# A gated graph network: the last step of the last pair by halves of the nodes, 1 - z ahead of tanh, one more turn on TensorE

## The chip, the cores and the metric

The kernel runs on one core of a Trainium2 chip. The metric is device time in microseconds for one execution. The core has TensorE (PE, with its weight loads shown apart as PEld), VectorE (DVE), ScalarE (ACT), GpSimd (POOL), and SyncE (SP), whose queue issues every DMA here. The profile records one execution; its span runs from the first to the last instruction.

## The reference, cut to what matters

x is 32 samples of 512 nodes with 128 features, adj a 512 x 512 matrix shared by all. Everything is in float32.

```python
# layer 0: powers of adj up to 3 (both adjacencies are the same adj)
x = layernorm(x + sum_k (adj^k @ x) @ W_k)
# layer 1: five steps of a gated update
h = x
for _ in range(5):
    m  = adj @ h                       # in_matrix and out_matrix are the same
    u3 = h @ u3_w.T + u3_b
    z  = sigmoid(cat(m, m) @ w3_w.T + w3_b + u3)
    r  = sigmoid(cat(m, m) @ w4_w.T + w4_b + u3)
    hv = tanh(cat(m, m) @ w5_w.T + w5_b + ((r * h) @ u5_w.T + u5_b))
    h  = (1 - z) * h + z * hv
out = layernorm(x + h)                 # x here is the output of layer 0
```

## The kernel before

The 32 samples are worked as 16 pairs (q = 0 to 15, b = 0 and 1 within a pair). A pair goes through layer 0 and then through five steps (s = 0 to 4) with its h kept turned, features on the partitions and 512 nodes along the free dimension, in a tile hT of 128 x 512. In each step PE makes u = u3 h (L978; ACT adds the bias, L983, into a uT buffer), then the product of the pair with adj. That product is one of Strassen's seven-product schemes: sums S of blocks of X on POOL (L501), seven products on PE (L514), each taken out of its bank by ACT (L375) or DVE (L379), into m. Then come the gates of each batch (function gates): m with w4, w3 and w5 on PE (L896), additions on DVE (L901, L908), sigmoids on ACT (L903, L910), rh = r h on DVE (L904), rh with u5 on PE into the bank of w5, tanh on ACT (L917), and h + z (hv - h) on DVE and POOL (L929, L931, L933).

For the next product h is needed with nodes on the partitions (X). Most steps turn it by DMA (function turn): a stream transpose of 32 x 32 blocks on DVE (L350), four puts to DRAM (L342), one fetch (L348). The X that comes so lies in blocks, and ACT (two) and POOL (one) copy parts of it into S (L494). ON_PE says how many of a pair's last steps turn h with four PE transposes (L293) and one ACT copy (L1030) instead: one for pair 14, two for pair 15. Where step 4 itself is such a step (pairs 14 and 15), the last update is "quick": 1 - z is a second sigmoid with scale -1 (L922), (1 - z) h and z hv are products on DVE (L924, L926), and function finish adds h0, (1 - z) h and z hv in one PSUM bank with 48 small matmuls for a pair (24 for a batch, L944, with the identity as one operand), which also turns them. Then norm takes the statistics of each of four node blocks on DVE (L304, L305), the scale on POOL (L308 to L313), applies it on ACT (L321; for the very last batch on DVE, L317, with a shorter POOL part), and one DMA stores the sample (L961; L1045 for the other pairs).

No order is written out by hand. Every operation is handed to a Plan with its engine, an estimated duration, the operations it comes after, the buffer slots it takes and gives back, and a key. Plan.run goes through time with these estimates, and whenever an engine is free, gives it the ready operation with the smallest key, provided that its slots are free; ties go to the one that became ready first. The order in which operations leave this run is each engine's instruction order. A pair's keys are KEYS[q] plus 30 plus LONG (19) per step plus an offset for the kind of work: product 0, u 5, gates 10 to 10.8, turning 15. TT_KEY is the key of a set of sums of adj blocks (TT, L243), made once near the start and used by the four-sample product in layer 0. Slots that matter below: 2 rh buffers, 6 uT buffers, 8 PSUM banks, 14 slots "inside", one of which a pair holds from the start of its five steps to their end.

Of the kernel before, what the change touches and what calls it, by code (L numbers as in the profile page):

```python
# [10 lines left out]
AF = mybir.ActivationFunctionType  # L11
ALU = mybir.AluOpType
# [3 lines left out]
NK = 4  # L16
N = NK * P
H = NK // 2
HN = N // 2
R = 32  # L20
NR = P // R
STEPS = 5
ON_PE = {14: 1, 15: 2}
KEYS = [-2.0, 20.0, 50.0, 76.0, 96.0, 132.0, 162.0, 176.0, 194.0, 222.0, 242.0, 278.0, 304.0, 334.0, 350.0, 366.0]
LONG = 19.0
TT_KEY = 33.0
SQ_KEY = 16.0
KEPT = 3
FIRST = 2
# [97 lines left out]
def gnn_resnorm_kernel(  # L127
# [17 lines left out]
    nc = tc.nc  # L145
    NP = x.shape[0] // 2
# [7 lines left out]
    def tiles(tag, n, shape=(P, N), pool=work):  # L154
# [3 lines left out]
        bank=tiles("bank", 8, pool=psum),  # L158
        d=tiles("d", 6, (NR, R, NR, P), dram),
# [8 lines left out]
        hT=tiles("hT", 8),  # L168
        X=tiles("X", 3),
        uT=tiles("uT", 6),  # L170
        rh=tiles("rh", 2),
        z=tiles("z", 3),
        m=tiles("m", 5),
        S=tiles("S", 2, (P, 7, H, P)),
        v=tiles("v", 5),
        two=[None] * 4,
        inside=[None] * 14,
    )
    plan = Plan(slots)

    def chunk(k):
        return slice(k * P, (k + 1) * P)
# [3 lines left out]
    ident = const.tile([P, P], F32, tag="ident", name="ident")  # L186
# [40 lines left out]
    for i, (a, b) in enumerate(((B12, B11), (B22, T[:, 0]), (B22, B12), (B21, T[:, 1]))):  # L227
        emit = lambda i=i, a=a, b=b: nc.vector.tensor_tensor(T[:, i], a, b, ALU.subtract)
# [4 lines left out]
    for i, n, of in (  # L233
# [6 lines left out]
        t = lambda j, i=i, n=n: TT[:, i : i + n, j, :]  # L240
        own = []
        for j, (a, b) in enumerate(((b12, b11), (b22, t(0)), (b22, b12), (b21, t(1)))):
            emit = lambda d=t(j), a=a, b=b: nc.vector.tensor_tensor(d, a, b, ALU.subtract)  # L243
            after = T_sums + own[:2]
# [21 lines left out]
    ready = []  # L266
# [16 lines left out]
    u3s, u5s = plain(u3, "u3s"), plain(u5, "u5s")  # L283
    b3s, b4s, b5s = plain(b3, "b3s"), plain(b4, "b4s"), plain(b5, "b5s")
    ub3s, ub5s = plain(ub3, "ub3s"), plain(ub5, "ub5s")
    hv_b = const.tile([P, 1], F32, tag="hv_b", name="hv_b")
# [8 lines left out]
    def norm(n, name, src_of, dst_of, after, give, key, by_dve=False):  # L295

        mv = small.tile([P, n, 2], F32, tag="mv", name=f"mv_{name}")
        rstd = small.tile([P, n], F32, tag="rstd", name=f"rstd_{name}")
        shift = small.tile([P, n], F32, tag="shift", name=f"shift_{name}")
        got = []  # L300

        def moments(i):
            st = small.tile([P, 6], F32, tag="st", name=f"st_{name}_{i}")
            nc.vector.bn_stats(st, src_of(i))  # L304
            nc.vector.bn_aggr(mv[:, i, :], st)  # L305

        def power():
            nc.gpsimd.tensor_scalar(rstd, mv[:, :, 1], EPS, None, ALU.add)  # L308
            if not by_dve:
                nc.gpsimd.tensor_scalar(shift, mv[:, :, 0], -1.0, None, ALU.mult)  # L310
            nc.gpsimd.tensor_tensor(rstd, rstd, mhalf[:, :n], ALU.pow)  # L311
            if not by_dve:
                nc.gpsimd.tensor_tensor(shift, shift, rstd, ALU.mult)  # L313

        def apply(i):
            if by_dve:
                nc.vector.tensor_scalar(  # L317
                    dst_of(i), src_of(i), mv[:, i, 0:1], rstd[:, i : i + 1], ALU.subtract, ALU.mult
                )
                return  # L320
            nc.scalar.activation(  # L321
                dst_of(i), src_of(i), AF.Identity, bias=shift[:, i : i + 1], scale=rstd[:, i : i + 1]
            )

        for i in range(n):
            got.append(plan("DVE", 0.48, lambda i=i: moments(i), after=after, key=key))
        p = plan("POOL", 1.2 if by_dve else 1.75, power, after=got, key=key)
        engine, us = ("DVE", 0.35) if by_dve else ("ACT", 0.5)
        over = []
        for i in range(n):  # L330
            ends = give if i == n - 1 else []
            over.append(plan(engine, us, lambda i=i: apply(i), after=[p] + over, give=ends, key=key))
        return over
# [89 lines left out]
    for km in range(NK):  # L423
        emit = lambda km=km: transposes(plan[f"ba{km}"], lambda k: at[:, k, chunk(km)])
        take = [("bank", f"ba{km}")] + ([("h0", f"an{km // H}")] if km % H == 0 else [])
        tr = plan("PE", 0.44, emit, after=at_in, take=take, key=SQ_KEY)
        emit = lambda km=km: nc.scalar.copy(an_of(km)[:, km % H], plan[f"ba{km}"])
# [7 lines left out]
    for i, (a, b, op) in enumerate(  # L435
# [7 lines left out]
        emit = lambda i=i, a=a, b=b, op=op: nc.vector.tensor_tensor(an_sum(i)(), a(), b(), op)  # L443
        take = [("h0", f"anS{i // H}")] if i % H == 0 else []
# [14 lines left out]
    t = lambda i: lambda: T[:, i]  # L459
# [9 lines left out]
    dst = lambda i, j: at2[:, i * H : (i + 1) * H, j * HN : (j + 1) * HN]  # L469
    whole = lambda bank: bank.rearrange("p (k c) -> p k c", k=H)  # L470
    give = [("h0", f"{t}{i}") for t in ("an", "anS") for i in range(2)]
# [6 lines left out]
    for i, (a, b, op) in enumerate(  # L478
# [7 lines left out]
        emit = lambda i=i, a=a, b=b, op=op: nc.vector.tensor_tensor(at2S[:, i], a, b, op)  # L486
# [399 lines left out]
            turned.append(plan("ACT", 0.59, emit, after=[tr], give=[("bank", bn)], key=key + 20))  # L886
        return [normed[0], normed[1]], [[turned[0]], [turned[1]]]

    def gates(name, m, h, after, u_done, quick, key):


        uT = f"uT{name}"
        pr, pz, ph = (f"b{g}{name}" for g in "rzh")
        rh, z = f"rh{name}", f"z{name}"

        mm = lambda dst, w, src, first, last: nc.tensor.matmul(  # L896
            plan[dst], lhsT=w, rhs=plan[src], start=first, stop=last
        )
        take = [("bank", pr), ("rh", rh), ("z", z)]
        p = plan("PE", 0.86, lambda: mm(pr, w4s, m, True, True), after=after + weights + [u_done], take=take, key=key)  # L900
        emit = lambda: nc.vector.scalar_tensor_tensor(plan[pr], plan[pr], b4s, plan[uT], ALU.add, ALU.add)  # L901
        r = plan("DVE", 0.75, emit, after=[p, u_done], key=key)
        r = plan("ACT", 0.59, lambda: nc.scalar.activation(plan[pr], plan[pr], AF.Sigmoid), after=[r], key=key)  # L903
        emit = lambda: nc.vector.tensor_tensor(plan[rh], plan[pr], plan[h], ALU.mult)  # L904
        r = plan("DVE", 0.69, emit, after=[r], give=[("bank", pr)], key=key)

        p2 = plan("PE", 0.86, lambda: mm(pz, w3s, m, True, True), after=[p], take=[("bank", pz)], key=key + 0.5)
        emit = lambda: nc.vector.scalar_tensor_tensor(plan[pz], plan[pz], b3s, plan[uT], ALU.add, ALU.add)  # L908
        pre_z = plan("DVE", 0.75, emit, after=[p2, u_done], give=[("uT", uT)], key=key + 0.5)
        emit = lambda: nc.scalar.activation(plan[z], plan[pz], AF.Sigmoid)  # L910
        zs = plan("ACT", 0.59, emit, after=[pre_z], give=[] if quick else [("bank", pz)], key=key + 0.5)

        emit = lambda: mm(ph, w5s, m, True, False)
        p3 = plan("PE", 0.86, emit, after=[p2], take=[("bank", ph)], give=[("m", m)], key=key + 0.7)
        emit = lambda: mm(ph, u5s, rh, False, True)
        p4 = plan("PE", 0.86, emit, after=[p3, r], give=[("rh", rh)], key=key + 0.8)
        emit = lambda: nc.scalar.activation(plan[ph], plan[ph], AF.Tanh, bias=hv_b)  # L917
        t = plan("ACT", 0.66, emit, after=[p4], key=key + 0.8)
        if quick:

            rest = f"rest{name}"
            emit = lambda: nc.scalar.activation(plan[rest], plan[pz], AF.Sigmoid, scale=-1.0)  # L922
            k = plan("ACT", 0.59, emit, after=[pre_z, zs], take=[("rh", rest)], give=[("bank", pz)], key=key + 0.6)
            emit = lambda: nc.vector.tensor_tensor(plan[h], plan[rest], plan[h], ALU.mult)  # L924
            k = plan("DVE", 0.69, emit, after=[k, r], give=[("rh", rest)], key=key + 0.7)
            emit = lambda: nc.vector.tensor_tensor(plan[z], plan[ph], plan[z], ALU.mult)  # L926
            return k, plan("DVE", 0.69, emit, after=[t, zs], give=[("bank", ph)], key=key + 0.8)

        emit = lambda: nc.vector.tensor_tensor(plan[ph], plan[ph], plan[h], ALU.subtract)  # L929
        t = plan("DVE", 0.69, emit, after=[t], key=key + 0.8)  # L930
        emit = lambda: nc.vector.tensor_tensor(plan[z], plan[ph], plan[z], ALU.mult)  # L931
        t = plan("DVE", 0.69, emit, after=[t, zs], give=[("bank", ph)], key=key + 0.8)
        emit = lambda: nc.gpsimd.tensor_tensor(plan[h], plan[z], plan[h], ALU.add)  # L933
        return plan("POOL", 1.27, emit, after=[t], give=[("z", z)], key=key + 0.8)

    def finish(q, b, name, h, parts, h0_of, after, key, done):

# [26 lines left out]
    def pair(q, key0):  # L964

        entered = plan("-", 0.0, lambda: None, take=[("inside", f"in{q}")], key=key0)
        after, h_done = layer0(q, key0, [entered])
        h0_of = lambda b: plan[f"h0{q}"][:, b]
        h = [f"hT{q}_{b}" for b in range(2)]
        X_of, turned = h0_of, False  # L970
        for s in range(STEPS):
            key = key0 + 30.0 + LONG * s
            name = f"{q}_{s}"
            last = s == STEPS - 1
            u_done = []
# [35 lines left out]
            for b in range(2):  # L1011
                nm = f"{name}_{b}"
                Xb = f"X{nm}"
                quick = last and not by_dma
                d = gates(nm, f"m{nm}", h[b], got[b], u_done[b], quick, key + 10)
                if quick:
                    finish(q, b, nm, h[b], d, h0_of, read[b], key + 15, done)
                    h_done.append(list(d))
# [91 lines left out]
```

## Time and profile before

| What | us |
|---|---|
| median of 4 runs | 1513.73 (1512.94 to 1514.61) |
| the profiled execution, its own time | 1513.94 |
| its span, first to last instruction | 1512.2 |
| PE busy | 1495.5 in 6582 instructions |
| DVE, POOL, ACT busy | 1022.4, 836.8, 750.2 |
| granted TensorE clock, mean over the span | 0.998 |
| last store of pair 13, first and last of pair 15 issued at | 1474.4, 1506.9, 1509.0 |

How to read it. A line of a timeline gives the start in us from the start of the span, the length, the engine, the line of the kernel, the operation, the tile written and the tiles read (buffer numbers left out), the shapes, and how many instructions were merged; in brackets, how long the engine stood idle before it and what ended that. A line of waits names the engine and the tile that waited, what it waited for, and then the total in us, the number of times, and the longest. A table by stretches gives from:to, the length, the busy time of PE, PEld, DVE, ACT and POOL with the number of instructions, the granted TensorE clock, the share of the DMA engines' time, and GB/s. The ends of matmuls are modelled, and a matmul is shown longer than the distance to the next start, since they are pipelined.

### The profile page before, as it was taken

How to read it: one execution, taken by the hardware profiler on the slowest of the kernel's cores; microseconds unless marked ns; L12 is line 12 of the kernel's file. 1: busy time of each engine (PE TensorE's matmuls, PEld its weight loads, DVE VectorE, ACT ScalarE, POOL GpSimd, SP SyncE). 2: the span in 40 equal slices, each digit the busy share in tenths (PEclk: the TensorE clock that was granted, in tenths of full speed). 3: DMA queues.
4: the chain of work that ended last, by engine and by line, in shares of the span. 5: the costliest groups of instructions: out<-in, count | busy, mean ns of one | idle time of the engine just before them, and what ended most of it. 6: DMA issues, size and time to landing. Idle time of an engine off the chain costs nothing.

```text
span 1512.2 us, 21120 instructions
## 1 busy us (share of the span) xinstructions
PE 1495.5 (99%) x6582; PEld 1044.4 (69%) x6582; DVE 1022.4 (68%) x2125; ACT 750.2 (50%) x1582; POOL 836.8 (55%) x1202
## 2 busy tenths in 40 slices
PE   8999999999999999999999999999999999999997
PEld 7877768676667767676676766676776776665665
DVE  5566675757776676767777577768477765767675
ACT  3354453554645554555455445546445544555454
POOL 3755743764545864766367454558374743553452
PEclk9999999999999999999999999999999999999999
DMA  3213333342433533343343243434243322342230
GB/s 96 71 56 105 103 91 100 86 117 86 124 91 88 142 100 100 94 119 87 98 116 91 82 125 91 131 91 121 75 126 98 92 63 78 101 114 70 76 79 36
DMA packets 167329, 143.97 MB, mean 95 GB/s; under 512 B 19120, under 2 KB 128688, under 8 KB 167216
## 3 DMA queue, kind: packets, MB, share of 16 engines
q1 hardware_dynamic: 167216, 142.62, 34.2%
q8 instruction: 52, 0.85, 0.3%
q14 instruction: 61, 0.50, 0.1%
HBM read 72.29 MB, written 70.25 MB: 94 GB/s over the span
## 4 chain that ended last, share of the span: by engine, by line
PE 94%; DMA 1%; issue 1%; DVE 1%; SPq 1%; POOL 1%; ACT 0%; ACTq 0%; POOLq 0%; DVEq 0%
PE bank L896 36%; PE bank L514 32%; PE bank L978 9%; PE bank L754 6%; PE bank L819 6%; PE bank L618 5%; PE bank L450 1%; PE bank L944 1%; SPq L342 1%; DMA v<-d 0%; DMA d<-v 0%; PE bank L293 0%; DMA xg<-in_x 0%; ACT h L321 0%; POOL rstd L311 0%
## 5 line engine op out<-in xcount | busy, mean ns | idle before, releaser
L933 POOL TENSOR_TENSOR hT<-z,hT 128x512 f32<-128x512 f32 x156 | 197.8, 1273 | 295.2 <-DVE z L931 281.0
L514 PE MATMUL bank<-T,S 128*128 128x256 f32 x1236 | 308.9, 380 | 0.5 <-ACT uT L375 0.5
L514 PEld LDWEIGHTS bank<-T,S 128*128 128x128 f32 x1236 | 229.9, 190 | 79.4 <-ACT m L375 29.8
L375 ACT COPY m<-bank 128x256 f32<-128x256 f32 x320 | 118.9, 371 | 272.8 <-PE bank L514 271.3
L514 PE MATMUL bank<-at,S 128*128 128x256 f32 x832 | 213.6, 379 | 0.9 <-ACT S L494 0.7
L514 PEld LDWEIGHTS bank<-at,S 128*128 128x128 f32 x832 | 154.5, 190 | 58.0 <-issue 35.3
L379 DVE TENSOR_TENSOR m<-bank,m 128x256 f32<-128x256 f32 x240 | 100.5, 419 | 136.0 <-PE bank L514 90.6
L929 DVE TENSOR_TENSOR bank<-bank,hT 128x512 f32<-128x512 f32 x156 | 108.1, 694 | 118.2 <-ACT bank L917 117.5
L896 PE MATMUL bank<-m,w4s 128*128 128x512 f32 x320 | 161.2, 593 | 0.0
L896 PE MATMUL bank<-rh,u5s 128*128 128x512 f32 x320 | 158.7, 592 | 0.0
L978 PE MATMUL bank<-hT,u3s 128*128 128x512 f32 x320 | 158.7, 593 | 0.0
L896 PE MATMUL bank<-m,w3s 128*128 128x512 f32 x320 | 156.6, 592 | 0.0
L896 PE MATMUL bank<-m,w5s 128*128 128x512 f32 x320 | 156.1, 592 | 0.0
L903 ACT ACTIVATE bank<-bank 128x512 f32<-128x512 f32 x160 | 93.3, 583 | 114.5 <-DVE bank L901 114.1
L901 DVE SCALAR_TENSOR_TENSOR bank<-bank,b4s,uT 128x512 f32<-128x512 f32 x160 | 119.9, 751 | 41.1 <-PE bank L896 39.2
L917 ACT ACTIVATE bank<-bank,hv_b 128x512 f32<-128x512 f32 x160 | 105.7, 662 | 82.1 <-PE bank L896 80.8
L983 ACT ACTIVATE uT<-bank,ub3s 128x512 f32<-128x512 f32 x160 | 109.4, 686 | 69.4 <-PE bank L978 68.6
L908 DVE SCALAR_TENSOR_TENSOR bank<-bank,b3s,uT 128x512 f32<-128x512 f32 x160 | 118.7, 752 | 14.5 <-PE bank L896 13.4
L910 ACT ACTIVATE z<-bank 128x512 f32<-128x512 f32 x160 | 95.0, 596 | 62.8 <-DVE bank L908 54.7
L350 DVE STREAM_TRANSPOSE v<-hT 128x512 f32<-128x512 f32 x154 | 107.3, 701 | 22.7 <-POOL hT L933 20.1
L904 DVE TENSOR_TENSOR rh<-bank,hT 128x512 f32<-128x512 f32 x160 | 108.0, 680 | 8.9 <-ACT bank L903 8.2
L931 DVE TENSOR_TENSOR z<-bank,z 128x512 f32<-128x512 f32 x156 | 105.0, 681 | 1.7
(173 smaller groups left out, 2437.2 us busy)
## 6 DMA issues: line engine op xcount, KB each, us to landing
d<-v SPq DMA_DIRECT2D x840, 64.0 KB, 1.8
X<-d SPq DMA_DIRECT2D x154, 256.0 KB, 2.7
v<-d SPq DMA_DIRECT2D x56, 256.0 KB, 2.8
xg<-in_x SPq DMA_DIRECT2D x32, 256.0 KB, 3.1
out<-h SPq DMA_DIRECT2D x32, 256.0 KB, 2.1
hd<-h SPq DMA_DIRECT2D x13, 512.0 KB, 3.8
h<-hd SPq DMA_DIRECT2D x13, 512.0 KB, 3.8
at<-in_adjT SPq DMA_DIRECT2D x4, 256.0 KB, 5.2
```

Source lines behind the costliest of these rows:

```text
L350: blocks = lambda: nc.vector.transpose(plan[f"v{name}"], src_of())
L375: return "ACT", COPY[cols], lambda src: nc.scalar.copy(dst(i, j), src)
L514: nc.tensor.matmul(dst, lhsT=left[:, k, :], rhs=right[:, k, :], start=(first and k == 0), stop=(last and k == H - 1), skip_group_check=True,)
L896: mm = lambda dst, w, src, first, last: nc.tensor.matmul(plan[dst], lhsT=w, rhs=plan[src], start=first, stop=last)
L901: emit = lambda: nc.vector.scalar_tensor_tensor(plan[pr], plan[pr], b4s, plan[uT], ALU.add, ALU.add)
L904: emit = lambda: nc.vector.tensor_tensor(plan[rh], plan[pr], plan[h], ALU.mult)
L908: emit = lambda: nc.vector.scalar_tensor_tensor(plan[pz], plan[pz], b3s, plan[uT], ALU.add, ALU.add)
L917: emit = lambda: nc.scalar.activation(plan[ph], plan[ph], AF.Tanh, bias=hv_b)
L929: emit = lambda: nc.vector.tensor_tensor(plan[ph], plan[ph], plan[h], ALU.subtract)
L933: emit = lambda: nc.gpsimd.tensor_tensor(plan[h], plan[z], plan[h], ALU.add)
L978: emit = lambda bn=bn, hb=h[b]: nc.tensor.matmul(plan[bn], lhsT=u3s, rhs=plan[hb], start=True, stop=True)
L983: emit = lambda bn=bn, uT=uT: nc.scalar.activation(plan[uT], plan[bn], AF.Identity, bias=ub3s)
```

## The change

Six things change.

- In the last step of pair 15 (new argument ends_here) the product with u5, tanh and the product with z are made in two halves of 256 nodes, each its own operation.
- There 1 - z is taken with a key ahead of tanh, into a free uT buffer instead of a rh buffer; (1 - z) h follows on DVE.
- A new function last_finish takes finish's place for pair 15: each half of the nodes is summed in a bank of its own, statistics start by halves (norm now accepts a list per half), and each sample is stored in two halves.
- Pair 14 turns h on PE after its last two steps instead of one (ON_PE).
- KEYS move: pairs 3 to 10 are 8 smaller, pairs 11 and 12 are 6 smaller, pairs 13 to 15 are 4 smaller; TT_KEY grows from 33 to 39; there are 16 "inside" slots.
- In every step of every pair the gates of batch 1 have a key 0.05 above those of batch 0.

```diff
-ON_PE = {14: 1, 15: 2}
-KEYS = [-2.0, 20.0, 50.0, 76.0, 96.0, 132.0, 162.0, 176.0, 194.0, 222.0, 242.0, 278.0, 304.0, 334.0, 350.0, 366.0]
+ON_PE = {14: 2, 15: 2}
+KEYS = [-2.0, 20.0, 50.0, 68.0, 88.0, 124.0, 154.0, 168.0, 186.0, 214.0, 234.0, 272.0, 298.0, 330.0, 346.0, 362.0]
 LONG = 19.0
-TT_KEY = 33.0
+TT_KEY = 39.0
...
-        inside=[None] * 14,
+        inside=[None] * 16,
...
         for i in range(n):
-            got.append(plan("DVE", 0.48, lambda i=i: moments(i), after=after, key=key))
+            ready = after[i * len(after) // n] if isinstance(after[0], list) else after
+            got.append(plan("DVE", 0.48, lambda i=i: moments(i), after=ready, key=key))
...
         p3 = plan("PE", 0.86, emit, after=[p2], take=[("bank", ph)], give=[("m", m)], key=key + 0.7)
+        if ends_here:
+
+            new = []
+            for g in range(2):
+                c = slice(g * HN, (g + 1) * HN)
+                emit = lambda c=c: mm(ph, u5s, rh, False, True, c)
+                p4 = plan("PE", 0.43, emit, after=[p3, r], key=key + 0.3 + 0.1 * g)
+                emit = lambda c=c: nc.scalar.activation(plan[ph][:, c], plan[ph][:, c], AF.Tanh, bias=hv_b)
+                t = plan("ACT", 0.43, emit, after=[p4], key=key + 0.3 + 0.1 * g)
+                emit = lambda c=c: nc.vector.tensor_tensor(plan[z][:, c], plan[ph][:, c], plan[z][:, c], ALU.mult)
+                new.append(plan("DVE", 0.42, emit, after=[t, zs], key=key + 0.3 + 0.1 * g))
+            plan("-", 0.0, lambda: None, after=new, give=[("bank", ph), ("rh", rh)], key=key)
+            rest = f"rest{name}"
+            emit = lambda: nc.scalar.activation(plan[rest], plan[pz], AF.Sigmoid, scale=-1.0)
+            k = plan("ACT", 0.59, emit, after=[pre_z, zs], take=[("uT", rest)], give=[("bank", pz)], key=key + 0.2)
+            emit = lambda: nc.vector.tensor_tensor(plan[h], plan[rest], plan[h], ALU.mult)
+            k = plan("DVE", 0.69, emit, after=[k, r], give=[("uT", rest)], key=key + 0.2)
+            return [k, k], new
...
+    def last_finish(q, b, name, h, parts, h0_of, after, key, done):
+
+        z = f"z{name}"
+        keep, new = parts
+        banks = [f"bt{name}{g}" for g in range(2)]
+        over = []
+        for g in range(2):
+
+            def summed(tile, turned, first, last, g=g):
+                for i in range(H):
+                    a = tile(g * H + i)
+                    nc.tensor.matmul(
+                        plan[banks[g]][:, chunk(i)],
+                        lhsT=a if turned else ident,
+                        rhs=ident if turned else a,
+                        start=(first and i == 0),
+                        stop=last,
+                        skip_group_check=True,
+                    )
+
+            emit = lambda summed=summed: summed(lambda k: h0_of(b)[:, k, :], False, True, False)
+            t = plan("PE", 0.22, emit, after=list(after), take=[("bank", banks[g])], key=key + 0.6)
+            emit = lambda summed=summed: summed(lambda k: plan[h][:, chunk(k)], True, False, False)
+            t = plan("PE", 0.22, emit, after=[t, keep[g]], key=key + 0.1)
+            emit = lambda summed=summed: summed(lambda k: plan[z][:, chunk(k)], True, False, True)
+            over.append([plan("PE", 0.22, emit, after=[t, new[g]], key=key)])
+        y = lambda k: plan[banks[k // H]][:, chunk(k % H)]
+        give = [("bank", bank) for bank in banks] + [("hT", h), ("z", z)]
+        normed = norm(NK, f"1_{2 * q + b}", y, lambda k: h0_of(b)[:, k, :], over, give, key + 0.2, b == 1)
+        for g in range(2):
+
+            def emit(g=g):
+                to = out[2 * q + b].rearrange("(p k) c -> p k c", k=NK)
+                nc.sync.dma_start(to[:, g * H : (g + 1) * H], h0_of(b)[:, g * H : (g + 1) * H])
+
+            done.append(plan("SP", 0.36, emit, after=normed[: (g + 1) * H], key=key, late=2.0))
...
-                d = gates(nm, f"m{nm}", h[b], got[b], u_done[b], quick, key + 10)
+                ends_here = quick and q == NP - 1
+                d = gates(nm, f"m{nm}", h[b], got[b], u_done[b], quick, key + 10 + 0.05 * b, ends_here)
+                if ends_here:
+                    last_finish(q, b, nm, h[b], d, h0_of, read[b], key + 10.3 + 0.05 * b, done)
+                    h_done.append(d[0] + d[1])
+                    continue
```

More of the change, by code (lines that the diff above doesn't have):

```diff
@@ L887, in layer0, with gates @@
         return [normed[0], normed[1]], [[turned[0]], [turned[1]]]
-    def gates(name, m, h, after, u_done, quick, key):
+    def gates(name, m, h, after, u_done, quick, key, ends_here=False):
         uT = f"uT{name}"
@@ L894, in gates, with mm @@
         rh, z = f"rh{name}", f"z{name}"
-        mm = lambda dst, w, src, first, last: nc.tensor.matmul(
-            plan[dst], lhsT=w, rhs=plan[src], start=first, stop=last
-        )
+        def mm(dst, w, src, first, last, c=slice(0, N)):
+            nc.tensor.matmul(
+                plan[dst][:, c], lhsT=w, rhs=plan[src][:, c], start=first, stop=last, skip_group_check=True
+            )
         take = [("bank", pr), ("rh", rh), ("z", z)]
@@ L934, in gates @@
         return plan("POOL", 1.27, emit, after=[t], give=[("z", z)], key=key + 0.8)
+    def last_finish(q, b, name, h, parts, h0_of, after, key, done):
[7 more added lines that the diff above has]
+                    a = tile(g * H + i)
+                    nc.tensor.matmul(
+                        plan[banks[g]][:, chunk(i)],
[4 more added lines that the diff above has]
+                        skip_group_check=True,
+                    )
+            emit = lambda summed=summed: summed(lambda k: h0_of(b)[:, k, :], False, True, False)
[12 more added lines that the diff above has]
+            done.append(plan("SP", 0.36, emit, after=normed[: (g + 1) * H], key=key, late=2.0))
     def finish(q, b, name, h, parts, h0_of, after, key, done):
```

## The prediction, made before the changed kernel ran

> **What bounds the kernel now.** I read the page's busy shares and chain first, then the busy time by stretches of the span, then the waits of PE, then the timeline of the last 20 us. The page:
>
> ```profile
> PE 1495.5 (99%) x6582; PEld 1044.4 (69%) x6582; DVE 1022.4 (68%) x2125; ACT 750.2 (50%) x1582; POOL 836.8 (55%) x1202
> PE 94%; DMA 1%; issue 1%; DVE 1%; SPq 1%; POOL 1%; ACT 0%; ACTq 0%; POOLq 0%; DVEq 0%
> ```
>
> PE is busy 99% of the span and 94% of the chain is PE. By stretches (from:to, length, then busy time of PE, PEld, DVE, ACT, POOL with instructions):
>
> ```profile
> 0.00:60.00 60.00, 53.10 (x323) 47.44 (x324) 36.10 (x84) 21.45 (x49) 29.47 (x47) 1.00 0.31 88
> 60.00:1480.00 1420.00, 1419.09 (x6136) 979.41 (x6135) 969.54 (x1990) 716.53 (x1509) 798.89 (x1140) 1.00 0.35 97
> 1480.00:1504.00 24.00, 23.35 (x127) 17.55 (x125) 14.11 (x40) 10.77 (x24) 5.66 (x12) 1.00 0.06 23
> 1504.00:1512.20 8.20, 0.00 (x0) 0.00 (x0) 2.68 (x12) 1.50 (x4) 2.77 (x6) 0.68 0.17 65
> ```
>
> PE's idle time is 6.9 us in the first 60, only 0.91 in the next 1420, 0.65 in the last 24 of its work, and 8.2 after its last product. In between, a saved wait of any other engine is worth nothing; an added PE instruction costs its whole time. PE's waits from 60 us on:
>
> ```profile
> PE bank L514 <- ACT S L494: 0.7, 1, 0.7
> PE bank L514 <- ACT m L375: 0.5, 1, 0.5
> PE bank L514 <- DVE m L379: 0.2, 1, 0.2
> ```
>
> Matmul ends are modelled, so a gap shows less than it costs: the 0.46 us gap at 1489.59 follows four 256-column matmuls that began at 1488.11 and normally pass in 0.86, and the next four take 0.97 to the following start: 0.62 + 0.11 = 0.73 lost. By that ratio the 0.91 + 0.65 us are worth at most 2.5 us (estimate).
>
> The tail, from the timeline:
>
> ```profile
> 1498.29 1.95 PE L944 MATMUL bank<-h,ident 128*128 128x128 f32 x16
> ...
> 1500.97 1.06 PE L944 MATMUL bank<-ident,z 128*128 128x128 f32 x8
> ...
> 1502.06 0.30 DVE L304 BATCH_NORM_STATS2 st<-bank 128x6 f32<-128x128 f32 x1 [1.31 <-PE bank L944]
> ...
> 1502.76 1.06 PE L944 MATMUL bank<-ident,z 128*128 128x128 f32 x8
> ...
> 1505.48 1.33 DVE L317 TENSOR_SCALAR h<-bank,mv,rstd 128x128 f32<-128x128 f32 x4
> 1505.65 0.22 POOL L308 TENSOR_SCALAR rstd<-mv 128x4 f32<-128x4 f32 x1 [0.43 <-DVE mv L305]
> ...
> 1506.85 2.50 SPq L961 DMA_DIRECT2D out<-h  x2
> 1507.48 1.50 ACT L321 ACTIVATE h<-bank,shift,rstd 128x128 f32<-128x128 f32 x4 [7.64 <-POOL shift L313]
> ```
>
> 48 summing matmuls run without a gap to 1503.82; eight statistics on DVE follow, 0.40 to 0.43 us each, to 1505.56; POOL makes the scale of batch 0 to 1507.45; ACT applies it to 1508.98; the last store is issued at 1509.01, and the span ends 3.2 us later. Batch 1 goes first, because its m is ready first.
>
> **Part by part.**
>
> *ON_PE, pair 14.* Its turn from step 3 to 4 leaves the DMA. Gone: two stream transposes (DVE, 0.70 each), eight puts and two fetches on SP's queue, two S copies on ACT (0.41) and one on POOL (0.40). Added: two copies on ACT (0.60) and eight PE transposes. Pair 15 already does the same:
>
> ```profile
> 1475.05 0.60 PE L293 MATMUL bank<-ident,hT 128*128 128x128 f32 x4
> 1475.49 1.02 PE L896 MATMUL bank<-m,w3s 128*128 128x512 f32 x2
> ```
>
> Four transposes take 0.44 us until the next start; two batches, 0.87 us. They fall where PE has no gap: **+0.87**, on the path. What it buys is an early X: the h of pair 14 is summed on POOL at 1442.12 and 1444.71, and S first reads both X at 1458.50; by PE (pair 15: h done 1473.43, X copied 1476.32) it takes 2.9 us. But PE did not wait for that X, so the gain is 0. On SP the puts of pair 13 that stood behind move up by up to ten issues (some 4 us); PE waits for none of them either.
> The Trainium skill ("TensorE: Matmul & The Clock Gate", Part 4: PE-mode transpose) puts a 128x128 transpose at about 275 ns in a kernel's context. This trace also shows 272 ns as one instruction's duration, but the starts are 0.11 us apart. By the page's figure the eight would cost 2.2 us; by the row 0.87.
>
> *KEYS, and 0.05 for batch 1.* These change no work, only the order in which the plan hands ready operations to the engines. Pairs 0 to 2 keep their keys, and the first of pair 3 in the first 60 us is the transpose of its x at 58.19, so the head's 6.9 us stay. From there the order is new everywhere. Below, at most the 2.5 us above can be won; what can be lost has no row, so I bound it by the longest chain without cover (rival 2, 5.7). I take 0, since the present order lost only 0.91 in 1420 us.
>
> *TT_KEY, inside.* The last TT sum ends at 29.59 us, the first DVE operation with a key between 33 and 39 (a norm of pair 1, a gate of pair 0) stands after 50: same order, 0. Slots 15 and 16 of "inside" matter only before a pair has left; the first store is at 317 us, and pair 14 enters long after: 0.
>
> *u5 by halves.* Four 256-column matmuls pass in 0.86 (L514), as two of 512 columns do: 0 on PE. Tanh by halves: no row for 256 columns; a 256-column copy takes 0.37 against 0.59, so some 0.44 (estimate), +0.22 per batch on ACT; the product with z 2 x 0.42 for 0.68, +0.16 on DVE. Cover: after u5 ends at 1498.29, PE has the 16 sums of h0 and then the sums of h until 1501.86; the last half of z is done near 1500.4. Were that cover gone, the late 0.4 us would cost its whole length.
>
> *1 - z in a uT buffer.* In a rh buffer it waited for u5, as both rh were in use: 1497.63. Now it can follow z, about 1496.0. Yet PE first asks for (1-z)h at 1500.08, and it was done at 1498.95 (second batch 1500.15, asked for at 1501.86): 0.
>
> *Sums, statistics, stores by halves.* Still 48 matmuls of 0.11 us: PE ends at 1503.8 as before. By the keys the four h0 halves go first (0.9), then h (0.4), then z (0.3), batch 0 ahead. h sums: batch 1 at 1500.08, batch 0 to 1501.86. z: batch 0 first half ends 1502.47, its second 1503.36, batch 1's last 1503.8. DVE: batch 0's statistics 1502.49 and 1502.92, then 1503.39 and 1503.82, done 1504.30; batch 1's four done 1505.93. POOL: batch 0 1504.39 to 1506.19 (1.80), batch 1 queued behind it, a new wait of 0.27, to 1507.55 (1.35, as at 1503.87 to 1505.22). DVE applies batch 1 to 1508.9 (1.33). Last store issued 1508.95: -0.06. SP issues four stores instead of two, 0.33 each and over 0.6 apart, so none queues. Half a store lands between 1.8 us (64 KB rows) and 2.0 (256 KB): -0.1. Sum **-0.2**. Ends: with batch 0 last in POOL and ACT, 1505.93 + 0.09 + 1.80 + 0.03 + 1.50 gives an issue at 1509.4, +0.35; with only two statistics after PE's last matmul, 1504.75 + 1.35 + 1.33 gives 1507.4, -1.6. I take -0.2, since all eight statistics need 3.3 us from about 1502.5 on, whichever order.
> The skill ("DMA: Bandwidth & Descriptors", the cost table under the SWDGE anatomy) calls about 2.0 us of a DMA fixed; by that a halved store lands no sooner and the sum is 0.1 worse.
>
> **Sum.** +0.87 - 0.2 + 0 = +0.67. The profiled execution took 1513.94 (span 1512.2 and 1.74 around it), 0.21 over the median; against the median 1513.73 the forecast is **1514.4**.
>
> **Rivals.**
>
> 1. *Faster.* The new order closes PE's small gaps (up to -2.5) and the halves work as meant (up to -1.6). Both whole: 1513.73 + 0.87 - 4.1 = 1510.5; half of each: 1512.5. For: the gap at 1489.59 lies in pair 15's last product, where nothing else was left. Against: the gaps are single, three different releasers, and DVE is as full in the tail as before.
> 2. *Slower.* Pair 14 runs ahead and leaves pair 15 without cover between its steps 3 and 4. The chain from the end of its last u5 (near 1470.0) through tanh, two on DVE, POOL (to 1474.66 for the second batch), transposes and copy needs about 5.7 us; now 11.3 us of work of pair 14 (gates 8 x 0.86, sums of h0) and of pair 15's own stand in it. It decides once less than 5.7 us of ready work is left there: wholly bare 1514.4 + 5.7 = 1520.1, half 1517.3. For: X of pair 14 comes some 9 us earlier, pairs 13 to 15 move only 4 against 8 of pairs 3 to 10. Against: pair 14's gates (key +10) still stand behind pair 15's of step 3.
> 3. *The halves do nothing* because the order stays one batch after the other: 1513.73 + 0.87 + 0.35 = 1515.0, within the forecast's own range.
>
> **How the numbers follow.** Forecast with rival 3, 0.63, own range 1512.9 to 1516.0; rival 1, 0.21, 1510.5 to 1512.9; rival 2, 0.16, 1516.0 to 1520.1. 0.2% is 3.0 us, about what a measurement of this kernel can tell from no change: faster is below 1510.7, slower above 1516.8. Faster 0.03 (rival 1's far end), slower 0.12 (three quarters of rival 2), same 0.85. The range 1511.6 to 1517.2 leaves out about 0.06 and 0.11.
>
> **What would show it.** Right: PE busy about 1 us more with 6594 instructions (8 transposes, 4 for the halved u5), PE idle from 60 us on still near 1.5, last matmul to span's end still near 8.2. Wrong: over 3 us of PE waits from 60 us on (rival 2 if they name X, L1030's copy or hT near the end); a tail under 7 us; head idle time other than 6.9.

## The result, and the profile after

| | us |
|---|---|
| before, median of 53 runs | 1513.11 (1511.13 to 1514.99) |
| changed, median of 33 runs | 1514.64 (1512.71 to 1517.30) |
| ratio, 95% interval | 1.0013 (1.0008 to 1.0017) |
| the changed kernel's profiled execution | 1514.13, span 1512.3 |

The changed kernel is slower by about 2.0 us by the ratio (1.2 to 2.6); the two medians alone differ by 1.5. The profiled spans are nearly equal, 1512.2 and 1512.3; that is chance, since the changed kernel's profile got through its first 40 us faster (see "Comparing two profiles"). First the page after, then its table by stretches with the columns explained above:

```profile
PE 1494.6 (99%) x6594; PEld 1045.2 (69%) x6594; DVE 1024.9 (68%) x2125; ACT 750.9 (50%) x1584; POOL 839.2 (55%) x1201
```

```profile
0.00:60.00 60.00, 53.95 (x339) 48.55 (x340) 37.24 (x86) 22.36 (x50) 34.31 (x51) 1.00 0.32 92
60.00:1480.00 1420.00, 1416.73 (x6125) 977.94 (x6124) 969.80 (x1987) 715.22 (x1504) 795.36 (x1133) 1.00 0.35 96
1480.00:1504.00 24.00, 23.89 (x133) 18.75 (x131) 14.71 (x42) 11.77 (x27) 6.59 (x12) 1.00 0.06 23
1504.00:1512.30 8.30, 0.00 (x0) 0.00 (x0) 3.19 (x14) 1.50 (x4) 2.93 (x6) 0.65 0.19 63
```

PE's idle time between 60 and 1480 us went from 0.91 to 3.27; from 1480 to 1504 it fell from 0.65 to 0.11. There are the twelve further instructions of the forecast. PE busy is 0.9 us lower, though more work was done; matmul ends are modelled and the first 60 us differ, so it can't show a difference of this size. The waits of PE from 60 us on:

```profile
PE bank L515 <- ACT m L376: 2.9, 3, 1.6
PE bank L619 <- DVE M L377: 0.2, 1, 0.2
PE bank L515 <- ACT S L495: 0.2, 1, 0.2
```

The longest of them in the timeline, with ACT's queue before it:

```profile
186.29 0.62 ACT L361 COPY xT<-v 128x512 f32<-128x512 f32 x1 [5.09 <-DMA v<-d]
...
186.81 0.36 ACT L376 COPY m<-bank 128x256 f32<-128x256 f32 x1
...
187.32 1.10 PE L515 MATMUL bank<-T,S 128*128 128x256 f32 x4 [1.58 <-ACT m L376]
```

ACT stood idle 5.09 us before a copy of a turned x, whose fetch had not landed. The copy of m that PE needed stood behind it in ACT's order and ran only after it. The wait of 1.1 us at 250 us has the same form; under the old order ACT also waited for such copies (4.0 us at 192.7), but PE had other work.

The tail:

```profile
1502.59 0.30 DVE L304 BATCH_NORM_STATS2 st<-bank 128x6 f32<-128x128 f32 x1 [1.49 <-PE bank L968]
...
1504.48 0.23 POOL L308 TENSOR_SCALAR rstd<-mv 128x4 f32<-128x4 f32 x1 [14.34 <-DVE mv L305]
...
1506.38 0.23 POOL L308 TENSOR_SCALAR rstd<-mv 128x4 f32<-128x4 f32 x1
...
1507.16 2.66 SPq L990 DMA_DIRECT2D out<-h  x4
1507.77 1.37 DVE L317 TENSOR_SCALAR h<-bank,mv,rstd 128x128 f32<-128x128 f32 x4 [1.77 <-POOL rstd L311]
```

PE's last product ends at 1503.89; the eight statistics end at 1505.99, POOL ends batch 1 at 1507.74, DVE applies it to 1509.14, and the last store is issued at 1509.43. From the last product to the span's end it takes 8.46 us, before 8.35.

**Comparing two profiles.** All kernels here have the same order up to the 189th matmul, and yet it starts at very different times. Before and after:

```profile
40.44 1.13 PE L514 MATMUL bank<-T,S 128*128 128x256 f32 x4 [0.46 <-ACT uT L375]
```

```profile
38.22 1.13 PE L515 MATMUL bank<-T,S 128*128 128x256 f32 x4 [0.46 <-ACT uT L376]
```

In the fourteen profiles it lies between 37.85 and 41.30. The pace of PE near the start makes most of this difference. Before, and in the changed kernel, each time four instructions of 256 columns and the one that follows them:

```profile
8.56 1.91 PE L514 MATMUL bank<-at,xg 128*128 128x256 f32 x4
10.27 1.06 PE L293 MATMUL bank<-ident,at 128*128 128x128 f32 x4
```

```profile
9.29 1.03 PE L515 MATMUL bank<-T,S 128*128 128x256 f32 x4
10.15 0.60 PE L293 MATMUL bank<-ident,at 128*128 128x128 f32 x4
```

The four take 1.71 us to the next start in the one and 0.86 in the other. Before, the distances halve at 11.9 us, and there the trace's first record of the full TensorE clock begins; in the changed kernel it begins at 8.1. Over the fourteen profiles it begins between 6.81 (e5) and 13.00 us (e6), and a line through them puts the 189th matmul 0.55 us later for each us. What sets that moment no run here shows. So I count from the 189th matmul on. "Work" is the number of PE instructions of each width times their usual distance to the next start (0.1105, 0.2155 and 0.4292 us for 128, 256 and 512 columns); "lost" is the rest up to the last product's end (9.44 in the least case); "tail" goes from there to the end of the span.

| kernel | ratio to before (95%) | from the 189th matmul | work | lost | tail |
|---|---|---|---|---|---|
| before | 1 | 1471.73 | 1452.92 | 10.46 | 8.35 |
| changed | 1.0013 (1.0008 to 1.0017) | 1474.13 | 1453.81 | 11.86 | 8.46 |
| e1 turn | 1.0004 (0.9996 to 1.0013) | 1472.51 | 1453.80 | 10.50 | 8.21 |
| e2 KEYS | 1.0047 (1.0033 to 1.0060) | 1479.12 | 1452.92 | 17.85 | 8.36 |
| e3 halves | 1.0003 (0.9994 to 1.0012) | 1471.34 | 1452.92 | 10.07 | 8.35 |
| e4 one batch, then the other | 0.9991 (0.9982 to 0.9999) | 1469.87 | 1452.92 | 10.03 | 6.91 |
| e5 KEYS and turn | 1.0027 (1.0017 to 1.0037) | 1474.47 | 1453.80 | 12.44 | 8.23 |
| e6 ten turns | 1.0065 (1.0052 to 1.0077) | 1480.15 | 1461.76 | 10.17 | 8.22 |
| e7 changed, later landing | 1.0015 (1.0006 to 1.0024) | 1473.29 | 1453.81 | 11.02 | 8.46 |
| e8 e4, later landing | 1.0017 (1.0008 to 1.0025) | 1473.68 | 1452.92 | 14.07 | 6.68 |
| e9 changed, one batch, then the other | 1.0001 (0.9992 to 1.0010) | 1472.12 | 1453.81 | 11.66 | 6.65 |
| e10 e4, one copy later | 0.9989 (0.9980 to 0.9998) | 1469.27 | 1452.92 | 9.44 | 6.91 |
| e11 ties | 1.0014 (1.0005 to 1.0022) | 1474.27 | 1452.92 | 13.01 | 8.34 |
| e12 e4 again | 0.9992 (0.9983 to 1.0001) | 1469.41 | 1452.92 | 9.57 | 6.91 |

e4 and e12 are one kernel, and their "lost" differs by 0.46, so smaller differences of one profile say nothing. The changed kernel's 2.40 us over before, counted so, are 0.89 of work, 1.40 lost to the order, and 0.11 of tail.

### The profile page after: what moved, and what is told of

It is laid out like the page before. It is cut to its first block, busy times and chain, and to the rows that moved or that the text cites. A ratio compares the mean times of both kernels' runs of the same rounds, so it can differ in the third digit from the quotient of the medians.

```text
span 1512.3 us, 21105 instructions
## 1 busy us (share of the span) xinstructions
PE 1494.6 (99%) x6594; PEld 1045.2 (69%) x6594; DVE 1024.9 (68%) x2125; ACT 750.9 (50%) x1584; POOL 839.2 (55%) x1201
## 4 chain that ended last, share of the span: by engine, by line
PE 94%; DMA 2%; SPq 2%; DVE 1%; ACT 0%; issue 0%; POOL 0%; POOLq 0%; DVEq 0%; ACTq 0%
PE bank L898 36%; PE bank L515 31%; PE bank L1036 9%; PE bank L755 6%; PE bank L820 5%; PE bank L619 5%; SPq L343 1%; DMA v<-d 1%; PE bank L451 1%; DMA d<-v 1%; PE bank L293 0%; PE bank L1002 0%; DMA xg<-in_x 0%; PE bank L968 0%; DVE v L351 0%
## 5 line engine op out<-in xcount | busy, mean ns | idle before, releaser
L898 PE MATMUL bank<-rh,u5s 128*128 128x512 f32 (+1 forms) x324 | 159.1, 587 | 0.0
```

The costliest lines, as they stand in the source:

```text
L898: nc.tensor.matmul(plan[dst][:, c], lhsT=w, rhs=plan[src][:, c], start=first, stop=last, skip_group_check=True)
```

## The experiments

With TT_KEY at 39 and 16 "inside" slots alone, the plan gives every engine the same instruction order as before. These two edits do nothing.

**e1, the turn alone.**

```diff
-ON_PE = {14: 1, 15: 2}
+ON_PE = {14: 2, 15: 2}
```

> The kernel before with one edit, pair 14 turned on TensorE after its last two steps. Theory (the sum of work): 8 more PE instructions, 0.87 us more of PE, PE idle from 60 us on as before (1.6 us, give or take 0.5), so +0.9 us, ratio 1.0006. Rival (the early X pays): the gap of 0.46 us in pair 15's last product goes and others with it, -0.5 us or less, ratio under 1.0000.

Work +0.88, lost +0.04; the gap of 0.46 us in pair 15's last product is still there. The ratio alone can't be told from 1, but it excludes a gain of over 0.6 us. With the old keys the early X buys nothing that can be seen.

**e2, KEYS alone.**

```diff
-KEYS = [-2.0, 20.0, 50.0, 76.0, 96.0, 132.0, ...
+KEYS = [-2.0, 20.0, 50.0, 68.0, 88.0, 124.0, ...
```

> The kernel before with the new KEYS alone. Theory (the new order puts ACT's copies of a turned x too early in its queue): PE idle between 60 and 1480 us goes from 0.9 to at least 2.5 us, by waits for ACT copies of m or UY that stand behind a copy xT<-v which waits for its DMA; +1.5 us, ratio 1.001. Rival (the ties of 0.05, not the keys, or chance): PE idle there stays at 0.9, give or take 0.5, ratio 1.0000.

Slower by 7 us (5 to 9), and neither theory had it: waits for ACT's copies grew, as the first one says, but they are the smaller part. The waits of PE from 60 us on begin so:

```profile
PE bank L293 <- POOL hT L933: 3.2, 1, 3.2
PE bank L514 <- ACT m L375: 1.8, 4, 0.7
PE bank L978 <- ACT hT L360: 0.9, 1, 0.9
```

and in the timeline:

```profile
1476.20 1.02 PE L896 MATMUL bank<-m,w5s 128*128 128x512 f32 x2
1480.42 1.12 PE L293 MATMUL bank<-ident,hT 128*128 128x128 f32 x4 [3.19 <-POOL hT L933]
1481.33 1.91 PE L896 MATMUL bank<-rh,u5s 128*128 128x512 f32 x2
```

This is rival 2 of the prediction: pair 15 bare between its steps 3 and 4. PE stands before pair 15's transposes, since pair 15's h comes late. One reason lies in DVE's order:

```profile
1476.41 0.76 DVE L908 SCALAR_TENSOR_TENSOR bank<-bank,b3s,uT 128x512 f32<-128x512 f32 x1 [1.85 <-PE bank L896]
1477.07 1.29 DVE L929 TENSOR_TENSOR bank<-bank,hT 128x512 f32<-128x512 f32 x2
```

The first is an addition of pair 14, for which DVE waited 1.85 us; the update of pair 15's h (L929) stands behind it, though the tanh that it needs was over at 1474.50. The wait of PE costs more than it shows: the four transposes then take 0.91 us to the next start instead of 0.44 (see the end). The profile is of the slowest of five runs (1521.82; the median is 1519.06), so the 7.4 us lost in it may be more than is usual.

**e3, the halves alone** (the changed kernel with old KEYS, ON_PE, TT_KEY and slots, and without the ties but in the last step).

```diff
-                d = gates(nm, ..., u_done[b], quick, key + 10 + 0.05 * b, ends_here)
+                d = gates(nm, ..., u_done[b], quick, key + 10 + 0.05 * b * ends_here, ends_here)
```

> The kernel before with the last step of pair 15 by halves alone (u5, tanh, product with z, 1 - z early, sums, statistics and stores by halves; old keys, no 0.05 elsewhere). Theory (eight statistics on DVE follow the sums whichever way they are cut): last matmul to span's end 8.2 to 8.5 us as before (8.4), 0 give or take 0.4 us. Rival (the halves work as meant): under 7.4 us there, -1 us or more.

Tail 8.35, as before; ratio 1.0003 with 1 well inside. The halves are worth nothing in this order.

**e4 and e12, one batch, then the other.** e3 with:

```diff
-            t = plan("PE", 0.22, emit, ...
+            t = plan("PE", 0.44, emit, ...
...
-    key + 10.3 + 0.05 * b
+    key + 10.3 + 0.05 * (1 - b)
...
-        normed = norm(..., over, give, key + 0.2, b == 1)
+        normed = norm(..., over, give, key + 0.2, b == 0)
```

(The gates' keys of this step are turned round in the same way.)

> The third kernel of this call with the sums of a half costed in the plan at 0.44 us instead of 0.22, and batch 1, whose m is ready first, ahead of batch 0 in the last step, so that PE makes all sums of batch 1 before those of batch 0. Theory (what the tail waits for is the order of the sums, not their size): batch 1's four statistics lie beside PE's sums of batch 0, only batch 0's last two follow PE, last matmul to span's end about 6.9 us, -1.5 us, ratio 0.9990. Rival (POOL and the store set the tail): 8.0 us or more there, under 0.4 us won.

> The fourth kernel of the first call once more, beside the kernel with one ACT copy moved. Theory: 0.9991 again (0.9985 to 0.9996), last matmul to span's end 6.9 us. Rival (its first ratio was chance): 0.9998 or more.

Tail 6.91 in both, ratios 0.9991 and 0.9992. In e4's timeline the first statistics start while PE still has half of its sums to do:

```profile
1498.41 0.29 DVE L304 BATCH_NORM_STATS2 st<-bank 128x6 f32<-128x128 f32 x1
1498.49 1.06 PE L968 MATMUL bank<-h,ident 128*128 128x128 f32 x8
...
1500.27 1.06 PE L968 MATMUL bank<-ident,z 128*128 128x128 f32 x8
...
1500.92 0.30 DVE L304 BATCH_NORM_STATS2 st<-bank 128x6 f32<-128x128 f32 x1 [0.80 <-PE bank L968]
```

Batch 1's four statistics lie beside PE's sums of batch 0, and batch 0's first statistic starts 0.41 us before PE's last sum is over. What the halves can be worth here is these 0.41 us and the 0.3 by which a half store lands sooner (estimate; see the next section); the rest of the 1.44 us of tail is the order of the batches. This order without halves was not run. Two things changed at once, the cost in the plan (0.22 us for four instructions that take 0.44) and which batch goes first, and no run parts them. By the order that the plan itself puts out, the cost is what matters: with it alone batch 0's sums all stand ahead of batch 1's of h and z, while with the batches turned round at the old cost the last sums of both still alternate.

**e5, KEYS and the turn together.**

> The kernel before with the new KEYS and pair 14 turned on TensorE, and nothing else. In the run with KEYS alone PE stood still 5.5 us between 1480 and 1500 us, 3.2 of it before pair 15's transposes, and the time was 1.0047 of before. Theory (the early X of pair 14 costs 0.87 us and is what covers pair 15 under the new keys): that wait is gone, PE idle from 60 us on is 2 to 4 us, ratio 1.001 to 1.002, 4 to 5 us less than KEYS alone. Rival (the cover comes from the order of ties or from the halves): the wait of about 3 us before pair 15's transposes stays, ratio 1.004 to 1.006.

The wait before the transposes is gone: pair 15's are there at once, between pair 14's gates.

```profile
1474.47 1.02 PE L896 MATMUL bank<-m,w4s 128*128 128x512 f32 x2
1475.33 0.60 PE L293 MATMUL bank<-ident,hT 128*128 128x128 f32 x4
1475.77 1.02 PE L896 MATMUL bank<-m,w3s 128*128 128x512 f32 x2
```

From the 189th matmul on, 4.65 us less than KEYS alone, with 0.88 more work; by the ratios 3.0 less. The ratio, 1.0027 (1.0017 to 1.0037), is above what I expected. Had the turn bought nothing, it would have been 1.0047 and 0.88 us, some 1.0053. The 5.5 us of my expectation was wrong: after KEYS alone PE's waits from 60 us on add up to 6.8, of which 3.7 lie between 1470 and 1500.

**e6, what a transpose costs.** e1 with each of pair 14's two sets of four transposes issued ten times:

```diff
-    emit = lambda bn=bn, hb=h[b]: transposes(plan[bn], lambda k: plan[hb][:, chunk(k)])
+    emit = lambda bn=bn, hb=h[b]: [transposes(plan[bn], lambda k: plan[hb][:, chunk(k)]) for _ in range(10 if q == 14 else 1)]
```

> The first kernel of the first call (pair 14 turned on TensorE, old keys) with each of its two sets of four transposes issued ten times over into the same bank. The same values come out. Theory (an instruction on a full PE costs its whole distance to the next start, 0.109 us): 72 more, +7.8 us over the single turn, ratio to before about 1.0057. Rival by a duration of 0.27 us each: +19.6 us, ratio 1.0135. Rival (the turn lies beside other work): under +3 us.

1480.15 - 1472.51 = 7.64 us for 72 transposes, 0.106 each; by the ratios, 9.2 us, whose intervals overlap 7.8. By the 275 ns of the Trainium skill ("TensorE: Matmul & The Clock Gate", Part 4: PE-mode transpose) it would have been 19.8 us (estimate). The trace has 272 ns too, as the duration of one; in a row on a full PE they cost the distance between starts.

**e7 and e8, the landing in the plan.** The changed kernel, and e4, with:

```diff
-        return plan("SP", 0.35, fetch, ..., key=key, late=2.8)
+        return plan("SP", 0.35, fetch, ..., key=key, late=6.5 if take[0][0] == "v" else 2.8)
```

> The changed kernel with one figure of the plan changed: the landing of the fetch of a turned x or h0 (v<-d) is reckoned at 6.5 us instead of 2.8, so that ACT's copies from it stand later in ACT's queue. Theory (the waits of PE at 187 and 250 us come from ACT copies of m that stand behind such a copy): both are gone, so is the one of 0.9 us near 51 us, PE idle between 60 and 1480 us falls from 3.3 to under 1.5 us, and the time by 2 us or more against the changed kernel, ratio to before 1.000. Rival (the DMA itself is late for PE, whatever stands on ACT): PE idle stays at 3 us or moves to waits for hT or xT; ratio 1.001 or more.

> The fourth kernel of the first call (old keys, pair 15's last step by halves, one batch after the other) with the same figure of the plan at 6.5 us. Theory: the tail keeps its 6.9 us, the wait near 51 to 53 us (0.9 to 1.1) goes, some of the 0.9 us after 60 too: 1 us under the fourth kernel, ratio to before 0.998 to 0.9985. Rival (a new order brings as many new waits as it removes): 0.999 or more.

Half a hit. In e7 the waits at 187 and 250 us are gone, as they should be if ACT's order made them (every engine's order is new here, so it is the rows above that show the cause); the one near 51 became one of 0.7 at 54. But PE's idle time between 60 and 1480 us fell only to 2.49, with new, smaller waits elsewhere, and by the ratios the time did not fall (1.0015 against 1.0013). e8 missed: the new order left pair 15 bare again, with a wait of 3.2 us for hT before its transposes.

**e10, one ACT copy moved.** e4 with the landing of pair 2's x alone at 5.0 us; PE's order does not change.

```diff
+        late=5.0 if name.startswith("x2_") else 2.8
```

> The fourth kernel with the landing of pair 2's turned x alone reckoned at 5.0 us: in the whole program one ACT copy (the second xT<-v) moves behind two copies UY<-bank; PE, POOL and SP keep their order. Theory (head of the line on ACT): PE's wait of 0.9 to 1.1 us near 51 to 53 us for ACT's UY goes to under 0.2, nothing else changes, 0.9 us under the fourth kernel, ratio to before about 0.9985. Rival (the wait is for the products themselves): the wait stays, same time as the fourth kernel.

PE's wait for UY, a tile of layer 0 (0.8 in e12), is gone, and a product 3.6 us further on waits instead:

```profile
PE bank L755 <- POOL S L502: 0.7, 1, 0.7
```

Lost 9.44 against 9.57 in e12, 0.9989 against 0.9992: no gain that can be told. Taking one wait away brought out another, on another engine.

**e11, the ties alone.**

```diff
-                d = gates(nm, f"m{nm}", h[b], got[b], u_done[b], quick, key + 10)
+                d = gates(nm, f"m{nm}", h[b], got[b], u_done[b], quick, key + 10 + 0.05 * b)
```

> The kernel before with the 0.05 between the batches' gates alone. Theory (an order at random among near equals, about as good as another): PE idle between 60 and 1480 us 0.5 to 2.5 us, pair 15 covered between its steps 3 and 4, ratio 0.9995 to 1.0010. Rival (the ties are what uncovers pair 15 or what saves it): a wait of 3 us for hT near 1480 us, ratio 1.003 or more, or a gain of over 1 us.

Neither expectation held. Pair 15 is covered, but PE idles 3.67 us between 60 and 1480 in many places (the longest wait is 0.9, at 325), and the ratio, 1.0014, is as large as the whole change's.

**e9, the change with e4's last step.**

> The changed kernel, whole, with the fourth kernel's last step (the sums of a half costed at 0.44 us in the plan, batch 1 ahead of batch 0). Theory (the tail is worth the same wherever it is put): last matmul to span's end 6.9 us against the changed kernel's 8.4, 1.5 us under the changed kernel, ratio to before 1.0003. Rival (its new order of the middle hides it): 1.0010 or more.

Tail 6.65, 1.0001 (0.9992 to 1.0010): the order of the sums gives back about what the rest of the change costs. e4 and e10, which leave keys and turn alone, are the fastest, by 0.1% (the interval of e12, which is e4 again, just reaches 1), and can't be told from each other.

## Why the prediction held, and where it failed

- *PE is the bound; the turn costs 0.87.* Right: 0.88 more work in e1, 0.89 in the changed kernel, and e6 has the price by itself.
- *The early X is worth 0.* Right under the old keys (e1), wrong for the change as a whole: under the new ones it takes away a wait before pair 15's transposes, 4.65 us net (e2 against e5). The rival "pair 15 bare" named the place and nearly the price (5.7 us wholly bare; e2 lost 7.4 in all), but I put it down to an early pair 14. It was the other way: an early pair 14 is what covers.
- *KEYS and ties: "I take 0".* This is the term that was mis-sized: 1.40 us more lost in the profile, where the waits of 1.58 and 1.13 us for ACT's copies are new and old ones of 0.7 and 0.5 are gone. I argued that the old order lost little, but that says nothing of a new one: the old order was a good one among those run here. KEYS lost 7.4 us more than the order they replaced, the ties 2.6, KEYS on top of the turn 1.9, the landing on top of e4 4.0; less was lost by the landing on top of the changed kernel (0.8), by the ties and halves on top of KEYS and turn (0.6), and hardly by one moved copy (0.1 to 0.6, where a repeat differs by 0.46). The parts don't add: e1, e2, e3 and e11 alone sum to +10.3 us from the 189th matmul, the whole has +2.4.
- *Head unchanged at 6.9.* Its order is unchanged; its time is not a constant (37.85 to 41.30 at the 189th matmul). The idle time came to 6.05, which I had named as a sign of being wrong; since it goes with the moment of the full clock, it tells nothing.
- *PE idle from 60 us on near 1.5, over 3 us of waits a sign of being wrong.* That sign came: idle 3.38, waits 3.3. They name m, M and S, not X or hT, so it is not rival 2 but the KEYS term above.
- *1 - z early, u5 and tanh by halves: 0.* Right: in e3 lost is 10.07 and tail 8.35.
- *Tail -0.2.* It came to +0.11. The order of sums and statistics was as worked out, the statistics' times within 0.1 us. POOL ended 0.19 later than worked out, DVE's four applications took 1.37 instead of 1.33, and "none queues" was wrong: SP issued a store at 1508.53 just after batch 1's first half was applied, and batch 0's second half, applied by 1507.83, only behind it at 1508.90, so the last store left at 1509.43, 0.29 after the data was ready. A half store landed in 1.7 to 1.8 us, a whole one in 2.0, so half a store does land sooner. The Trainium skill ("DMA: Bandwidth & Descriptors", the cost table under the SWDGE anatomy) has beside its fixed 2.0 us a part of bytes over 436 GB/s, fitted to DMAs that GpSimd issues; my line on it left that part out. With it a whole store would take 2.6 us and a half 2.3 (estimates): the difference is about the measured one, and the constant is too large for these stores, which SyncE issues.

So 1514.4 came within 0.3 of 1514.64 partly by luck. I forecast +0.67 and the change was +1.5 to +2.0, more than twice that, because one term was 1.4 us too small; the lower median of before in the later runs (1513.11 against 1513.73) took 0.6 off again. What held is the mechanism: PE is the bound, its added work is paid in full, and the halves do nothing in this order (rival 3).

## What to carry to other kernels

Where one engine is 99% busy, count the instructions that a change adds to it, at their distance to the next start, and then ask what becomes of the order: here an order made by a list scheduler and already nearly without gaps got a little better (by about 1 us at most) or much worse (7.4), and the changes to it did not add up. A tail is set by what is left after the last product, so try one batch's sums wholly ahead of the other's before cutting anything in halves. A plan's cost of an operation (0.22 for 0.44) helps to decide whether it sees that.

## What the runs showed of the hardware that was not expected

A wait of 3.2 us on PE is paid for twice. In e2 the granted TensorE clock falls to half towards its end and stays there behind it (PEclk is the number after POOL's busy time and count):

```profile
1476.00:1480.40 4.40, 1.23 (x3) 0.19 (x1) 3.89 (x7) 1.78 (x4) 1.30 (x2) 0.95 0.12 45
1480.40:1483.40 3.00, 2.98 (x7) 1.92 (x8) 0.54 (x1) 0.71 (x2) 2.39 (x2) 0.50 0.00 0
1483.40:1487.00 3.60, 3.60 (x18) 2.24 (x17) 2.71 (x4) 2.28 (x5) 1.54 (x3) 1.00 0.00 0
```

In the middle stretch PE is busy and does 7 instructions in 3.0 us, at clock 0.50. The trace's record of half clock lasts from 1479.98 to 1483.39 and begins inside the wait, before PE's next instruction. The Trainium skill ("TensorE: Matmul & The Clock Gate", HAM oscillation) warns of gaps over about 3.4 us; here a wait shown as 3.19 was enough, in e8 too, where the half clock begins 1.1 us after PE's next instruction. By the usual distance between starts, which leaves the modelled ends out, both waits are 3.4 (3.36 and 3.35), so alone they don't contradict that figure. The end of the spans shows the same with nothing to wait for: in the fourteen profiles the record falls to half clock between 2.1 (e1) and 5.2 us (e4) after PE's last product, so 2.1 us without work can be long enough, and over 5 us can pass first. Past the first 60 us no other wait of PE here is longer than 1.6 us, and none of those brought it; what decides is not shown.

And the first 40 us differ by up to 3.4 us between executions of the same order, with the moment at which the full clock begins, which is more than this change is worth: before two profiles are subtracted, an instruction that both reach by the same order has to be found and counted from.
